# Building the filter's polynomials for two units in one block of matmuls

## The chip, the cores and the metric

The kernel runs on one core of a Trainium2 chip. Times are microseconds of device time from the start to the end of one execution; the median of three executions is given. The engines of the core are TensorE (PE, with its weight loads PEld), VectorE (DVE), ScalarE (ACT), GpSimd (POOL) and SyncE (SP), which issues most DMAs.

## What is computed

Two layers act on images of shape (4, 512, 512, 16), both on group-normalised input and with a residual. The first is a convolution through the frequency domain, the second a 3x3 cosine-similarity convolution. The change lies in how the filter of the first is made, for each of 16 x 16 pairs of input channel i and output channel j:

```python
a = jnp.pad(denumerator, ((0, 0), (0, 0), (1, 0), (1, 0)), constant_values=1.0)
b = jnp.pad(numerators, ((0, 0), (0, 0), (0, 0), (1, 0), (1, 0)), constant_values=0.0)
H_truncated = jnp.fft.rfft2(b, s=(l1, l2)) / jnp.fft.rfft2(a, s=(l1, l2))
h_truncated = jnp.fft.irfft2(H_truncated, s=(l1, l2))
H = jnp.fft.rfft2(h_truncated, s=(2 * l1, 2 * l2))
H_full = h0 + H[0]
```

Both a and b are polynomials of 9 x 9 coefficients in two variables, evaluated at 512 x 512 frequencies (256 of the second are kept). Their quotient is the filter, h0 is added by way of b + h0 a, and the result goes to the taps in space and on to 1024 x 1024 frequencies.

## The kernel before

The program has four stages in a row: the filter (`filter_phase`), the forward transform of the images, the product in the frequency domain, and the last stage with the inverse transform and the second layer. Beside the filter stage runs `image_stats`, statistics of the images on VectorE.

The filter stage works through a list `work` of 1024 units: output channel j, half h of the second frequency (128 of 256), input channel i, and kp, two of four blocks of 128 of the first frequency. The loop over v (L445) takes one unit a step and works on four units at once, each at a later point:

- `polynomials` (L321) makes a and b of unit v. First `quad` (L303) has multiplied the coefficients of four channels with the powers of the first frequency (L313) and copied the products to u (L315): a tile of 128 rows for a and one for b, in which each channel has a group of 32 rows (18 of them used: real and imaginary parts of nine coefficients). Channel i lies in group i % 4 of the tile for a, and in group (i % 4) ^ 1 of that for b. L329 multiplies those 18 rows by the powers of the second frequency, e2, for two blocks k: four matmuls a unit, each of 128 x 256 outputs, into two PSUM tiles pab0 (a) and pab1 (b). A float32 matmul is two instructions in the profile, so a unit has eight. ACT copies both tiles to SBUF (ab, L335) and squares a (sq, L337).
- `square` (L341, GpSimd) adds the squares to |a|^2 (dn). `product` multiplies b by a elementwise (m, L347, VectorE), takes the reciprocal of dn (L348, VectorE) and multiplies the crossed parts (x, L350 and L351, GpSimd).
- `terms` (L355, L356, GpSimd) puts real and imaginary part of the product together in m; `quotient` (L361, VectorE) multiplies them by 1/|a|^2 into sp and, for h = 0, puts in the special column z (L364).
- `taps` (L372) multiplies sp by dinv into PSUM (pg, four matmuls, eight instructions), and ACT copies the two parts into the stage tiles st (L377). After i = 15, kp = 1, SyncE stores the two stage tiles to memory (L383).

Each step also advances `odd` (L389) by one part: two matmuls (four instructions, L417) for the odd rows of a channel j that is already stored, whose copy is VectorE's (L423) and ACT's (L425) in turn, with loads ahead (L403) and stores (L426) by SyncE.

Buffers decide who may run ahead: PSUM has four banks for pab (L239), two a unit; two for pg, two for pt, pu and pz together; SBUF has two of each of ab, sq, dn, m and sp, one of x, and three stage tiles for the two of each j and h. The order of instructions on each engine is the framework's scheduler's, which starts from the written order and moves what is ready ahead: the statistics, written one of two bn_stats a step, stand at some eight a unit in places.

The step of the loop that calls these functions, and its functions, follow with line numbers.

Of the kernel before, what the change touches and what calls it, by code (L numbers as in the profile page):

```python
# [40 lines left out]
F32 = mybir.dt.float32  # L41
# [5 lines left out]
P = 128  # L47
N = 512
B = 4
C = 16  # L50
# [135 lines left out]
def load_const(nc, pool, cst, name, shape=None):  # L186
    src = cst[name]
    t = pool.tile(list(src.shape), F32, name=f"c_{name}")
    nc.sync.dma_start(out=t, in_=src)
    return t  # L190
# [38 lines left out]
def filter_phase(tc, cst, h0, num, den, g_d, beside):  # L229
    nc = tc.nc  # L230
    with ExitStack() as ctx:
# [7 lines left out]
        ps_ab = ctx.enter_context(tc.tile_pool(name="f_psab", bufs=4, space=PSUM))  # L239
# [4 lines left out]
        e2 = load_const(nc, cp, cst, "e2").rearrange("p (s h n) -> p s h n", s=2, h=2)  # L244
# [58 lines left out]
        def quad(sa, sb, iq):  # L303

            us = []
            for n, s in enumerate((sa, sb)):
                pu = ps_t.tile([P, N], F32, name=f"pu{n}", tag="t")  # L310
                for i in range(4):
                    at = 32 * (i ^ n)
                    nc.tensor.matmul(pu[at : at + 32], s[:, 4 * iq + i], e1, start=True, stop=True)  # L313
                u = wt.tile([P, N], F32, name=f"u{n}")
                nc.scalar.copy(u, pu)  # L315
                us.append(u)
            return us

        def polynomials(w):  # L321

            pp = [ps_ab.tile([P, 2, 2, P], F32, name=f"pab{n}", tag="ab") for n in range(2)]
            for k in range(2):
                k1 = (2 * w["kp"] + k) * P
                for n in range(2):
                    at = 32 * (w["i"] % 4 ^ n)
                    q = slice(at, at + 18)
                    nc.tensor.matmul(  # L329
                        pp[n][:, k].rearrange("p c n -> p (c n)"),  # L330
                        w["us"][n][q, k1 : k1 + P], e2[q, n, w["h"], :], start=True, stop=True,
                    )
            w["ab"] = [ew.tile([P, 2, 2, P], F32, name=f"ab{n}") for n in range(2)]
            for n in range(2):
                nc.scalar.copy(w["ab"][n], pp[n])  # L335
            w["sq"] = ew.tile([P, 2, 2, P], F32, name="sq")
            nc.scalar.activation(w["sq"], w["ab"][0], AF.Square)  # L337

        def square(w):
            w["dn"] = ew.tile([P, 2, P], F32, name="dn")  # L340
            nc.gpsimd.tensor_add(w["dn"], w["sq"][:, :, 0], w["sq"][:, :, 1])  # L341

        def product(w):

            a, b = w["ab"]
            w["m"] = ew.tile([P, 2, 2, P], F32, name="m")
            nc.vector.tensor_mul(w["m"], b, a)  # L347
            nc.vector.reciprocal(w["dn"], w["dn"])  # L348
            w["x"] = ew.tile([P, 2, 2, P], F32, name="x", bufs=1)
            nc.gpsimd.tensor_mul(w["x"][:, :, 0], b[:, :, 0], a[:, :, 1])  # L350
            nc.gpsimd.tensor_mul(w["x"][:, :, 1], b[:, :, 1], a[:, :, 0])  # L351

        def terms(w):
            m, x = w["m"], w["x"]
            nc.gpsimd.tensor_add(m[:, :, 0], m[:, :, 0], m[:, :, 1])  # L355
            nc.gpsimd.tensor_sub(m[:, :, 1], x[:, :, 1], x[:, :, 0])  # L356

        def quotient(w):
            sp = w["sp"] = ew.tile([P, 2, 2, P], F32, name="sp")
            for c in range(2):  # L360
                nc.vector.tensor_mul(sp[:, :, c], w["m"][:, :, c], w["dn"])  # L361
            if w["h"] == 0:
                kp = w["kp"]
                nc.vector.tensor_copy(sp[:, :, :, 0], w["z"][:, 2 * kp : 2 * kp + 2, :, w["i"]])  # L364

        def taps(w):

            kp, i, st = w["kp"], w["i"], w["st"]
            pg = ps_g.tile([P, 2, 2, 2 * 64], F32, name="pg")
            for k in range(2):  # L370
                for c in range(2):
                    nc.tensor.matmul(  # L372
                        pg[:, k].rearrange("p a x -> p (a x)"), w["sp"][:, k, c, :],
                        dinv[:, 2 * kp + k, c, :], start=(c == 0), stop=(c == 1),
                    )
            for a in range(2):
                nc.scalar.copy(  # L377
                    st[a][:, :, i].rearrange("p (q k x) -> p k q x", q=2, k=4)[:, 2 * kp : 2 * kp + 2],
                    pg[:, :, a].rearrange("p k (q x) -> p k q x", q=2),
                )  # L380
            if i == C - 1 and kp == 1:
                for a in range(2):
                    nc.sync.dma_start(  # L383
                        out=dram(g_d[w["h"]], None, a * G_ROW // 2 + w["j"] * 8 * C,
                                 [C * 8 * C, 64], [1, 8 * C]),
                        in_=st[a].rearrange("p (r e) i -> p r (e i)", e=8),
                    )
# [44 lines left out]
        def odds():  # L432

            for j in range(C):
# [2 lines left out]
                yield from odd(j)  # L437

        work = [dict(j=j, h=h, i=i, kp=kp)
                for j in range(C) for h in range(2) for i in range(C) for kp in range(2)]  # L440
        done = [0]
        rest = odds()
        polys = {0: weights(0)}
        us = quad(*polys[0][:2], 0)
        for v in range(len(work) + 3):  # L445
            next(rest)
            if v % 64 == 32 and v < len(work) - 64:
                polys[v // 64 + 1] = weights(v // 64 + 1)
            if v < len(work):
                w = work[v]  # L450
                if v % 8 == 0 and v:
                    us = ahead
                w["us"], w["z"] = us, polys[w["j"]][2]
                polynomials(w)
                if v % 8 == 4 and v + 4 < len(work):
                    g = (v + 4) // 8
                    ahead = quad(*polys[g // 8][:2], g % 4)
            first, second, third = (work[v - k] if 0 <= v - k < len(work) else None for k in (1, 2, 3))
            if first:
                square(first)  # L460
            if second:
                terms(second)
            if first:
                product(first)
            if second:
                quotient(second)
            if third:
                if third["i"] == 0 and third["kp"] == 0:
                    st = [stp.tile([P, N, C], F32, name=f"st{a}", tag="st") for a in range(2)]
                third["st"] = st  # L470
                taps(third)
                done[0] += 1
                third.clear()
            if v % 2:
                next(beside, None)
# [831 lines left out]
def body(tc, ins, cst, out):  # L1307
    g_d = [tc.dram_tile([P, G_ROW + PITCH], F32, name=f"g_d{r}") for r in range(4)]
    x_d = [tc.dram_tile([P, X_ROW + PITCH], F32, name=f"x_d{r}") for r in range(4)]
    y_d = [tc.dram_tile([P, Y_ROW + PITCH], F32, name=f"y_d{r}") for r in range(4)]  # L1310
    yw_d = [tc.dram_tile([C, N, N], F32, name=f"yw_d{b}") for b in range(B)]
    t_d = [[tc.dram_tile([N, P, C], F32, name=f"t_d{b}_{w}") for w in range(4)] for b in range(B)]
    with tc.tile_pool(name="s_mv", bufs=2 * B) as mp:
        mvs = []
        with tc.tile_pool(name="s_in", bufs=1) as xp:
            beside = image_stats(tc, xp, mp, ins["x"], mvs)
            filter_phase(tc, cst, ins["L0_conv_h0"], ins["L0_conv_numerators"][0],
                         ins["L0_conv_denumerator"], g_d, beside)
            for _ in beside:
                pass  # L1320
        forward_phase(tc, cst, ins["x"], mvs, x_d)
    conv_phase(tc, cst, g_d, x_d, y_d)
    last_phase(tc, cst, ins["x"], y_d, yw_d, t_d, ins["L1_conv_kernel"], ins["L1_conv_bias"],
               ins["L1_conv_radius"], out)
# [30 lines left out]
```

## Time and profile before

| | us |
|---|---|
| median of three runs | 19007.57 (19006.79 to 19023.34) |
| the profiled execution itself | 19054.31 |
| its span, first to last instruction | 19052.5 |
| last reciprocal of the filter stage (L348) starts at | 5669.8 |
| busy in the span: PE, DVE, ACT, POOL | 17293.1, 11398.8, 9747.4, 11564.3 |
| mean granted clock of TensorE in the span | 0.957 of full speed |

Busy times are sums over the whole span, in which four stages with different limits lie one behind the other. What an edit in the filter stage is worth has to be read from that stage alone: the same columns for a stretch of it, the order of time of each engine in it, and the waits. A timeline line has start, duration, engine, line of the program, operation, outputs and inputs by the program's names, shapes, and the number of instructions merged; in brackets the idle time of the engine before it, and what ended that. A busy TensorE is not a TensorE at its peak: matmuls are pipelined, so distances between starts are used here, not durations.

### The profile page before, as it was taken

How to read it: one execution, taken by the hardware profiler on the slowest of the kernel's cores; microseconds unless marked ns; L12 is line 12 of the kernel's file. 1: busy time of each engine (PE TensorE's matmuls, PEld its weight loads, DVE VectorE, ACT ScalarE, POOL GpSimd, SP SyncE). 2: the span in 40 equal slices, each digit the busy share in tenths (PEclk: the TensorE clock that was granted, in tenths of full speed). 3: DMA queues.
4: the chain of work that ended last, by engine and by line, in shares of the span. 5: the costliest groups of instructions: out<-in, count | busy, mean ns of one | idle time of the engine just before them, and what ended most of it. 6: DMA issues, size and time to landing. Idle time of an engine off the chain costs nothing. (4 is left out here: it accounts for less than half of the span.)

```text
span 19052.5 us, 536690 instructions
## 1 busy us (share of the span) xinstructions
PE 17293.1 (91%) x227020; PEld 12605.2 (66%) x227020; DVE 11398.8 (60%) x23961; ACT 9747.4 (51%) x17871; POOL 11564.3 (61%) x12445
## 2 busy tenths in 40 slices
PE   8899999999999988898888888888888888979999
PEld 5455555555554457777777777777777776868888
DVE  8877777777763335555555555555555554347656
ACT  4455555555552235555555555555555553107777
POOL 7577777777771126666666666666666664127655
PEclk7899999999999999999999999999999999999999
DMA  3755455555557668888888888888888887796321
GB/s 100 206 153 148 137 150 150 146 139 149 149 151 223 187 211 320 323 322 324 320 322 317 322 327 317 322 324 323 320 325 323 321 320 282 268 321 210 131 72 62
DMA packets 2918658, 4543.39 MB, mean 238 GB/s; under 512 B 117442, under 2 KB 2086300, under 8 KB 2809374
## 3 DMA queue, kind: packets, MB, share of 16 engines
q1 hardware_dynamic: 2686062, 3768.91, 58.5%
q0 software_dynamic: 174896, 605.89, 8.3%
q10 hardware_dynamic: 55296, 134.24, 2.1%
q8 instruction: 1789, 29.31, 0.6%
q14 instruction: 615, 5.04, 0.1%
HBM read 3031.23 MB, written 1477.31 MB: 237 GB/s over the span
## 5 line engine op out<-in xcount | busy, mean ns | idle before, releaser
L783 PE MATMUL pg<-c_dg,g 64*128 64x128 f32 x32832 | 2842.9, 291 | 320.9 <-ACT gh L683 159.5
L799 PE MATMUL pm<-xe,gh 128*32 128x64 f32 x131328 | 2403.4, 222 | 576.2 <-issue 353.1
L799 PEld LDWEIGHTS pm<-xe,gh 128*32 128x32 f32 x131328 | 2012.8, 110 | 1180.2 <-issue 996.4
L783 PEld LDWEIGHTS pg<-c_dg,g 64*128 64x128 f32 x32832 | 2283.2, 190 | 662.7 <-issue 262.5
L372 PE MATMUL pg<-c_dinv,sp 128*128 128x256 f32 x8192 | 2278.4, 426 | 294.3 <-ACT st L377 193.8
L828 DVE TENSOR_TENSOR z<-zq,pz 128x256 f32<-128x256 f32 x2052 | 862.0, 420 | 2617.2 <-ACT zq L827 2534.6
L348 DVE RECIPROCAL dn<-dn 128x256 f32<-128x256 f32 x1024 | 1790.8, 1749 | 778.3 <-POOL dn L341 778.0
L372 PEld LDWEIGHTS pg<-c_dinv,sp 128*128 128x128 f32 x8192 | 1609.9, 207 | 946.8 <-ACT st L377 215.3
L681 DVE COPY gh<-pg 128x512 f32<-128x512 f32 x2046 | 1410.5, 689 | 1294.1 <-PE pg L783 1289.6
L417 PE MATMUL pt<-ev_in,c_todd 128*128 128x512 f32 x4096 | 1970.1, 606 | 45.6 <-DMA ev_in<-g_d 27.0
L752 POOL TENSOR_TENSOR xu<-xe,c_late 128x256 f32<-128x256 f32 x2052 | 1393.4, 705 | 856.3 <-ACT xe L683 832.3
L335 ACT COPY ab<-pab 128x512 f32<-128x512 f32 x2048 | 1104.2, 592 | 1130.1 <-POOL m L355 333.3
L683 ACT COPY yf<-pm 128x512 f32<-128x512 f32 x2046 | 1210.5, 592 | 919.0 <-PE pm L799 904.3
L377 ACT COPY st<-pg 128x256 f32<-128x256 f32 x2048 | 1072.6, 623 | 1024.0 <-PE pg L372 619.3
L763 ACT COPY xe<-xl 64x1024 f32<-64x1024 f32 x513 | 538.8, 1050 | 1877.0 <-POOL xl L754 1877.0
L350 POOL TENSOR_TENSOR x<-ab,ab 128x256 f32<-128x256 f32 x1024 | 875.8, 855 | 933.6 <-ACT ab L335 907.0
L1208 PE MATMUL pc<-l_band,xn 128*128 128x160 f32 (+3 forms) x9024 | 1374.8, 309 | 65.0 <-DVE e_o L1255 64.0
L683 ACT COPY gh<-pg 128x512 f32<-128x512 f32 x2058 | 1201.2, 584 | 402.0 <-PE pg L783 393.6
L820 PE MATMUL pz<-c_ident,yf 128*128 128x128 f32 x8208 | 1378.2, 291 | 27.2 <-issue 25.4
L1208 PEld LDWEIGHTS pc<-l_band,xn 128*128 128x128 f32 x9024 | 1218.8, 197 | 224.7 <-issue 147.2
L329 PEld LDWEIGHTS pab<-c_e,u 18*128 18x128 f32 x8192 | 723.5, 188 | 809.5 <-ACT st L377 452.5
L417 PEld LDWEIGHTS pt<-ev_in,c_todd 128*128 128x128 f32 x4096 | 806.8, 198 | 669.9 <-issue 514.6
(195 smaller groups left out, 33846.4 us busy)
## 6 DMA issues: line engine op xcount, KB each, us to landing
xe<-xf_d SPq DMA_DIRECT2D x1026, 1536.0 KB, 10.3
g<-g_d SPq DMA_DIRECT2D x511, 1024.0 KB, 9.9
g_d<-st SPq DMA_DIRECT2D x64, 4096.0 KB, 34.3
ev_in<-g_d SPq DMA_DIRECT2D x1024, 256.0 KB, 4.8
g_d<-ot SPq DMA_DIRECT2D x1024, 256.0 KB, 2.9
xf_d<-xe POOLq DMA_DIRECT2D x513, 448.0 KB, 8.3
xf_d<-xl POOLq DMA_DIRECT2D x513, 448.0 KB, 5.3
x_d<-xo SPq DMA_DIRECT2D x128, 1024.0 KB, 5.1
```

The source lines that it names most:

```text
L335: nc.scalar.copy(w["ab"][n], pp[n])
L348: nc.vector.reciprocal(w["dn"], w["dn"])
L372: nc.tensor.matmul(pg[:, k].rearrange("p a x -> p (a x)"), w["sp"][:, k, c, :], dinv[:, 2 * kp + k, c, :], start=(c == 0), stop=(c == 1),)
L377: nc.scalar.copy(st[a][:, :, i].rearrange("p (q k x) -> p k q x", q=2, k=4)[:, 2 * kp : 2 * kp + 2], pg[:, :, a].rearrange("p k (q x) -> p ...
L417: nc.tensor.matmul(pt, todd[:, c, kc, hh * P : hh * P + P], ev[:, kc, c], start=(kc == 0), stop=(kc == 1),)
L681: nc.vector.tensor_copy(dst, src)
L683: nc.scalar.copy(dst, src)
L752: nc.gpsimd.tensor_mul(u[:, :, h, c], xe[:, :, h, 1 - c], bc(late[:, 1 + c], 2, [P, F, 2]))
L783: nc.tensor.matmul(pg[c][:, j % 4], g[half, j], dg[half], start=True, stop=True)
L799: nc.tensor.matmul(pm[32 * q : 32 * q + 32, g % 8], gh[:, f].rearrange("p c j -> p (c j)"), xe[:, :, f].rearrange("p t h c k -> p t (h c k ...
L820: nc.tensor.transpose(pz[:, t % 4].rearrange("p v q x -> p (v q x)"), y[:, at].rearrange("p g x -> p (g x)"), ident)
L1208: nc.tensor.matmul(pc[:, lo:hi, :].rearrange("p w j -> p (w j)"), xns[q][:, h * P + dh : h * P + dh + P], bands[dh][:, o : o + hi - lo, :] ...
```

## The change

The work list is put in another order: channels i and i ^ 2 stand side by side, and kp is outside of them. At every even step, `polynomials` now takes two units, allocates all four pab tiles, and issues their eight matmuls for k = 0 and then k = 1, in each k the two of the first unit and the two of the second. By the places of the rows, i, i ^ 1, i ^ 2 and i ^ 3, these four lie in the four groups of 32 rows. What came after the matmuls, the copies and the square on ACT, is a function `evict` of its own, called for one unit at every step, as before.

```diff
--- before.py
+++ after.py
@@ -318,19 +318,26 @@
-        def polynomials(w):
-            pp = [ps_ab.tile([P, 2, 2, P], F32, name=f"pab{n}", tag="ab") for n in range(2)]
+        def polynomials(pair):
+            for w in pair:
+                w["pp"] = [ps_ab.tile([P, 2, 2, P], F32, name=f"pab{n}", tag="ab") for n in range(2)]
             for k in range(2):
-                k1 = (2 * w["kp"] + k) * P
-                for n in range(2):
-                    at = 32 * (w["i"] % 4 ^ n)
-                    q = slice(at, at + 18)
-                    nc.tensor.matmul(
-                        pp[n][:, k].rearrange("p c n -> p (c n)"),
-                        w["us"][n][q, k1 : k1 + P], e2[q, n, w["h"], :], start=True, stop=True,
-                    )
+                for w in pair:
+                    k1 = (2 * w["kp"] + k) * P
+                    for n in range(2):
+                        at = 32 * (w["i"] % 4 ^ n)
+                        q = slice(at, at + 18)
+                        nc.tensor.matmul(
+                            w["pp"][n][:, k].rearrange("p c n -> p (c n)"),
+                            w["us"][n][q, k1 : k1 + P], e2[q, n, w["h"], :], start=True, stop=True,
+                        )
+        def evict(w):
             w["ab"] = [ew.tile([P, 2, 2, P], F32, name=f"ab{n}") for n in range(2)]
+            pp = w.pop("pp")
             for n in range(2):
                 nc.scalar.copy(w["ab"][n], pp[n])
             w["sq"] = ew.tile([P, 2, 2, P], F32, name="sq")
@@ -437,7 +444,8 @@
                 yield from odd(j)
         work = [dict(j=j, h=h, i=i, kp=kp)
-                for j in range(C) for h in range(2) for i in range(C) for kp in range(2)]
+                for j in range(C) for h in range(2) for i2 in range(0, C, 2) for kp in range(2)
+                for i in (i2 // 4 * 4 + i2 // 2 % 2, i2 // 4 * 4 + i2 // 2 % 2 + 2)]
         done = [0]
         rest = odds()
         polys = {0: weights(0)}
@@ -451,7 +459,11 @@
                 if v % 8 == 0 and v:
                     us = ahead
                 w["us"], w["z"] = us, polys[w["j"]][2]
-                polynomials(w)
+                if v % 2 == 0:
+                    pair = work[v : v + 2]
+                    pair[1]["us"] = us
+                    polynomials(pair)
+                evict(w)
                 if v % 8 == 4 and v + 4 < len(work):
                     g = (v + 4) // 8
                     ahead = quad(*polys[g // 8][:2], g % 4)
```

## The prediction

> **What bounds the kernel now.** The change lies in the filter stage alone, which the busy times in stretches place in the first 5700 us of the 19052.5 us span. I read its stretches first, then TensorE's timeline in one undisturbed stretch, then that of GpSimd, then the waits. The columns of the stretches are: stretch, length, busy us and instructions of PE, weight loads, DVE, ACT, POOL, granted clock, DMA share, GB/s.
> ```profile
> 110.00:400.00 290.00, 249.88 (x998) 160.64 (x996) 260.70 (x454) 142.83 (x284) 230.60 (x289) 0.72 0.32 87
> 1000.00:5600.00 4600.00, 4386.40 (x18754) 2602.75 (x18752) 3471.05 (x4454) 2601.71 (x4889) 3544.93 (x4412) 0.95 0.53 147
> 2104.71:2137.63 32.92, 32.92 (x141) 20.16 (x140) 25.18 (x32) 20.33 (x38) 27.52 (x34) 1.00 0.40 115
> 2137.63:2145.87 8.24, 8.24 (x37) 4.42 (x37) 6.34 (x7) 4.18 (x8) 7.83 (x12) 0.79 0.19 56
> ```
> From 1000 to 5600 us TensorE is busy 95%, no other engine over 77%. The trace has 849 reciprocals (one a unit) in it, so a unit takes 4600/849 = 5.42 us on average. The third line is seven units without a disturbance: 32.92/7 = 4.70 us each, TensorE busy throughout.
>
> TensorE's timeline (start, us, what) shows what fills 4.70 us, and, where the work list runs out, what a unit costs without its polynomials:
> ```profile
> 2109.41 1.13 PE L329 MATMUL pab<-c_e,u 18*128 18x256 f32 x8
> 2110.47 1.99 PE L372 MATMUL pg<-c_dinv,sp 128*128 128x256 f32 x8
> 2112.30 1.88 PE L417 MATMUL pt<-ev_in,c_todd 128*128 128x512 f32 x4
> 2114.11 1.13 PE L329 MATMUL pab<-c_e,u 18*128 18x256 f32 x8
> ...
> 5667.37 1.88 PE L417 MATMUL pt<-ev_in,c_todd 128*128 128x512 f32 x4
> 5669.09 1.89 PE L372 MATMUL pg<-c_dinv,sp 128*128 128x256 f32 x8
> 5670.81 1.88 PE L417 MATMUL pt<-ev_in,c_todd 128*128 128x512 f32 x4
> 5672.53 1.89 PE L372 MATMUL pg<-c_dinv,sp 128*128 128x256 f32 x8
> ```
> Start to start: polynomials 1.06, taps 1.83, odd rows 1.81, together 4.70. Without polynomials 1.72 + 1.72 = 3.44 us. So a block of polynomials costs TensorE 4.70 - 3.44 = 1.26 us, 0.20 of it in the neighbours' starts. Inside the block the trace has the eight instructions start at 2109.412, .418, .732, .738, .948, .954, 2110.163 and .170: four rounds of two that start 6 to 7 ns apart, the rounds 0.32, 0.216 and 0.216 us apart.
>
> The next limit is GpSimd:
> ```profile
> 2107.13 1.17 POOL L350 TENSOR_TENSOR x<-ab,ab 128x256 f32<-128x256 f32 x1 [1.93 <-ACT ab L335]
> 2108.26 0.74 POOL L351 TENSOR_TENSOR x<-ab,ab 128x256 f32<-128x256 f32 x1
> 2108.95 0.73 POOL L341 TENSOR_TENSOR dn<-sq 128x256 f32<-128x256 f32 x1
> 2109.63 0.74 POOL L355 TENSOR_TENSOR m<-m 128x256 f32<-128x256 f32 x1
> 2110.44 0.73 POOL L356 TENSOR_TENSOR m<-x 128x256 f32<-128x256 f32 x1
> 2111.83 0.82 POOL L350 TENSOR_TENSOR x<-ab,ab 128x256 f32<-128x256 f32 x1 [0.67 <-ACT ab L335]
> ```
> Its five operations go through without a pause and then wait for the copy of the next polynomials, which comes 0.07 us behind TensorE. From the start of x to the end of m it takes 4.04 us here and 4.14 and 4.29 in the next two units: 4.16, or 4.24 with the 0.08 us to the next start. GpSimd thus has only about 0.46 us of slack in a unit of 4.70.
>
> The waits from 1000 to 5600 us name what makes 4.70 into 5.42:
> ```profile
> POOL x L350 <- ACT ab L335: 753.3, 591, 11.3
> ACT st L377 <- DMA g_d<-st: 213.6, 27, 10.0
> PE pg L372 <- ACT st L377: 169.0, 27, 8.5
> ```
> Every 32 units the output stage waits about 8 us for a store, and all engines behind it (0.25 us a unit). Every eighth unit has the products of the next four channels (L313): 6.55 us at full clock, 8.24 in the fourth stretch above at a clock of 0.79.
>
> **What the Trainium skill says.** TensorE: Matmul & The Clock Gate, Part 3 (Packing small matmuls): matmuls on different groups of 32 rows run at once, start about 4 ns apart, and four such tiles of K=32, N=512 were measured 3.07 times as fast. The trace agrees for two row groups (6 to 7 ns). For four it shows only column groups: the L313 matmuls start at 2099.218, .225, .232, .238. Four row groups no line here shows. TensorEngine Tiling (Array Packing), Key Properties: a change of tiling mode drains the engine. The trace agrees: the last odd-row matmul to the first polynomial is 0.52 us where the next odd-row one would come at 0.43. GPSIMD Engine Reference, Key points: GpSimd shares its SBUF interfaces with VectorE, and contends with instructions of two SBUF inputs. The trace agrees: VectorE's quotient product (L361) has a minimum of 353 ns and a maximum of 991. The Clock Gate page, Part 1: the clock drops to half after windows of little activity and returns with it; here 0.72 from 110 to 400 us, where TensorE has no odd rows to do.
>
> **The change part by part.** *One block for two units.* 16 instructions in one block in place of two blocks of 8. If four row groups start together, it has four rounds as before and 2 x 6.5 ns more: a pair costs 4.703 + 3.44 + 0.013 = 8.16 us in place of 9.41. TensorE gains 1.25 us a pair, 0.62 a unit. The same 16 weight loads per pair lie within the block (eight take 0.73 of 1.13 us now, and loads in different row groups overlap). If only two start together, four more rounds of 0.216 come back, and 1.25 - 0.86 = 0.39 us a pair is left. That is the lower bound, for the drain is saved in any case; the upper is 1.25. I take 1.25.
>
> *Four banks at a time.* The pool has four banks and a pair takes all, so the block waits for the copies of both units of the pair before. Behind that wait on TensorE are the taps and odd rows; ACT's tap copies wait for them, and VectorE for its next free sp. With E the end of a block: ACT copies the first unit to E + 1.14, squares it to E + 1.8, copies taps to about E + 3.1, and copies the second unit to about E + 4.2, once GpSimd has released the older ab. TensorE wants the banks at E + 7.1 (8.16 - 1.06). Cover 2.9 us: cost nothing. If the scheduler puts the second copy behind the tap copy of the next unit, it ends about E + 7.6 and a pair loses 0.6 us, 0.3 a unit; that is the bound above. Below nothing it can also go: the second unit's polynomials wait in PSUM already, so GpSimd gets them without waiting for TensorE.
>
> *GpSimd becomes the limit.* TensorE's 4.08 us a unit is below GpSimd's 4.24. Its operations, VectorE's and ACT's are the same in number. I take 4.30: 4.24 and a little for more collisions with VectorE, whose quotient would fall beside the next x. Bounds: 4.08 (GpSimd's unhindered five times 0.73 would allow it) and 4.70 (nothing). The early stage, where TensorE is not the limit, went at some 4.8 us a unit, but with half clocks and statistics on VectorE; this speaks for the upper side.
>
> *Eighth units and stores.* The eighth unit's extra 1.85 us stays on TensorE: 0.23 a unit, 4.31 in all, so it remains on the path partly; I put 0.06 a unit as hidden. The 8 us for a store stay. The order of channels (i and i ^ 2 side by side) changes no instruction count: the quads still change every eighth unit, i = 15, kp = 1 is still last and issues the two stores, and no DMA is moved past another on SP, ACT or POOL. Cost nothing: only the order inside the quad differs.
>
> *The sum.* In units 160 to 1023 (from 1000 us on): 864 x (4.70 - 4.30) = 346, and 864 x 0.06 = 52. In the first 160, where VectorE does the statistics (609 of 700 us busy from 300 to 1000), about 0.03 us each, 5. Together 403, say 400 us. The later stages only start sooner. The profiled execution took 19054.31 us (span 19052.5 and 1.8 around it), 47 us or 0.25% over the median 19007.57; the difference is taken from both: 18654 for such an execution, 18610 for the median.
>
> **The rivals.**
> *VectorE and GpSimd bind earlier*, at 4.50 us a unit: 864 x 0.20 = 173, with some 15 more: 18820. For: the early stage's 4.8, VectorE's 991 ns when contended. Against: three GpSimd cycles of 4.04 to 4.29 in this very stage.
> *The whole saving arrives*: GpSimd goes at 4.08, and 864 x 0.62 = 536 and 15 more: 18460. For: an unhindered cycle is 5 x 0.73 = 3.65 with small gaps. Against: collisions are there already.
> *Four groups don't start together*: 0.39 us a pair, 0.19 a unit, 864 x 0.19 = 164: 18840. For: only two were seen. Against: four column groups do.
> *Slower by the clock*: TensorE has gaps at the pair's block, waiting for the fourth bank, and the clock halves. One such stretch costs 8.24 - 6.55 = 1.69 us now (the taps take 3.50 us in place of 1.99). Once in each pair: 8.16 + 1.69 = 9.85 against 9.41, 0.22 a unit, 864 x 0.22 = 190 slower: 19200. It decides from 1.25/1.69 = 0.74 halvings a pair. For: 0.72 in the early stage. Against: at 4.30 TensorE still works 95% of a unit, and today's halvings follow gaps near 1 us.
>
> **How the numbers follow.** Forecast 0.52 (18610, with its own range 18500 to 18740), earlier bound 0.18, whole saving 0.12, two at a time 0.06, clock 0.12. The range 18430 to 18880 takes in the first four; left out are the clock and some 0.06 of tails. A measurement of this kernel tells about 0.2% (38 us) from no change. Within it I put 0.02 of the earlier bound and 0.03 of the clock: same 0.05. Slower is 0.09, faster 0.86.
>
> **What would show it.** Right: 16 L329 instructions a block, in four rounds of four about 7 ns apart, a block of about 1.15 us every two units; GpSimd's wait for ab near nothing; units of about 4.3 us between disturbances; store waits as before. Wrong: eight rounds; blocks that wait for ab copies; clock below 0.9 from 1000 to 5600 us; GpSimd cycles of 4.5 us or more.

## The result and the profile after

The changed kernel takes 19053.78 us (median of 20 executions, 19011.07 to 19099.3) beside 19009.13 us of the kernel before (20 executions, 18967.88 to 19045.35): a ratio of 1.002 with a 95% interval of 1.0013 to 1.0027, so slower by 0.2%. The forecast was 18610, and its range ended at 18880.

The profiled execution of the changed kernel took 19023.83 us (span 19022.1), 30 us under its median; that of the kernel before was 45 us over its own. Spans are therefore compared here for the filter stage alone. The busy times in stretches, with the columns used before (stretch, length, PE, weight loads, DVE, ACT, POOL, clock, DMA share, GB/s):
```profile
110.00:400.00 290.00, 213.00 (x1004) 134.02 (x1003) 259.75 (x465) 148.41 (x290) 227.01 (x288) 0.77 0.35 94
1000.00:5600.00 4600.00, 4094.07 (x18733) 2409.82 (x18732) 3716.36 (x4545) 2522.52 (x4887) 3635.89 (x4413) 0.92 0.53 148
```
From 1000 to 5600 us TensorE is busy 292 us less than before (89% of the stretch, not 95%), with the same number of instructions to within 0.2%. VectorE is busy 245 us more. Of these, 22 us are 80 instructions of the statistics, which in the kernel before had ended by 1000 us; the rest is that operations changed in length: one instruction of sp takes 821 ns in the mean (574 before), while m takes 699 (868 before) and the copy of z 190 (370 before). GpSimd is busy 91 us more for the same number of operations. The stretch holds 847 reciprocals where it held 849, so nothing of TensorE's gain has come out.

TensorE's timeline shows the new block:
```profile
2505.31 1.15 PE L333 MATMUL pab<-c_e,u 18*128 18x256 f32 x16
...
2513.67 1.15 PE L333 MATMUL pab<-c_e,u 18*128 18x256 f32 x16
...
2516.69 1.98 PE L424 MATMUL pt<-ev_in,c_todd 128*128 128x512 f32 x4
2519.34 2.34 PE L379 MATMUL pg<-c_dinv,sp 128*128 128x256 f32 x8 [0.68 <-DVE sp L368]
```
Sixteen instructions take 1.15 us where eight took 1.13, and they start in four rounds of four (the first at 2505.307, .314, .321 and .327, 6 to 7 ns apart as two groups were before): the four groups of rows do start together. But in the last line TensorE stands still 0.68 us, and what it waits for is VectorE's sp. GpSimd's and VectorE's timelines of the same time tell why:
```profile
2513.36 0.73 POOL L357 TENSOR_TENSOR x<-ab,ab 128x256 f32<-128x256 f32 x1
2514.05 0.91 POOL L358 TENSOR_TENSOR x<-ab,ab 128x256 f32<-128x256 f32 x1
2515.38 1.24 POOL L348 TENSOR_TENSOR dn<-sq 128x256 f32<-128x256 f32 x1 [0.42 <-DVE sp L368]
2516.58 0.72 POOL L362 TENSOR_TENSOR m<-m 128x256 f32<-128x256 f32 x1
2517.38 0.73 POOL L363 TENSOR_TENSOR m<-x 128x256 f32<-128x256 f32 x1
...
2520.21 1.24 POOL L348 TENSOR_TENSOR dn<-sq 128x256 f32<-128x256 f32 x1 [0.43 <-DVE sp L368]
```
```profile
2513.49 1.74 DVE L368 TENSOR_TENSOR sp<-m,dn 128x256 f32<-128x256 f32 x2
2515.34 0.69 DVE L354 TENSOR_TENSOR m<-ab,ab 128x512 f32<-128x512 f32 x1
2515.95 0.69 DVE L430 COPY ot<-pt 128x512 f32<-128x512 f32 x1
2516.65 1.75 DVE L355 RECIPROCAL dn<-dn 128x256 f32<-128x256 f32 x1
2518.32 1.74 DVE L368 TENSOR_TENSOR sp<-m,dn 128x256 f32<-128x256 f32 x2
...
2521.48 1.75 DVE L355 RECIPROCAL dn<-dn 128x256 f32<-128x256 f32 x1 [0.62 <-POOL dn L348]
```
GpSimd no longer waits for ab in such units. It waits 0.42 us before dn, for sp (L368): dn has two buffers, and the one that is due is still read by the quotient of the unit two before. VectorE does a reciprocal, then the quotient of the unit before it. So there is a ring: dn starts at 2515.38, its reciprocal at 2516.65 (1.27 later), the quotient of the unit before at 2518.32 (1.67 later), and the next dn when that is over, at 2520.21 (1.89 later). Together 4.83 us, more than TensorE's 4.70 of before. VectorE's own work is not what sets this pace: in the unit shown it has no pause, but in the next one, whose odd-row copy is ACT's, it stands still 0.62 us for dn (the last line), and from reciprocal to reciprocal that unit takes 4.83 us too. Two of the three terms are stretched: the two instructions of sp, which run beside the two x, take 1.74 us (one of them by itself took at least 353 ns), and dn, which runs beside VectorE's m, takes 1.24 (0.73 by itself). Over the stretch from 1000 to 5600 us the median of one sp instruction went from 411 to 881 ns, and that of dn from 727 to 1237 ns (shortest, median and longest in ns; the kernel before first):
```profile
L361 DVE TENSOR_TENSOR sp<-m,dn x1698: 353/411/991, 1001.0 to 5597.5; 128x256 f32<-128x256 f32 x189
L341 POOL TENSOR_TENSOR dn<-sq x849: 714/727/1321, 1002.3 to 5599.1; 128x256 f32<-128x256 f32 x170
L368 DVE TENSOR_TENSOR sp<-m,dn x1695: 348/881/2356, 999.7 to 5598.2; 128x256 f32<-128x256 f32 x189
L348 POOL TENSOR_TENSOR dn<-sq x848: 716/1237/1249, 1005.3 to 5599.2; 128x256 f32<-128x256 f32 x170
```

The waits from 1000 to 5600 us confirm it for the whole stage:
```profile
POOL x L357 <- ACT ab L342: 477.4, 123, 11.7
...
POOL dn L348 <- DVE sp L368: 263.3, 593, 4.5
...
ACT st L384 <- DMA g_d<-st: 206.4, 27, 9.7
```
```profile
POOL dn L341 <- DVE sp L361: 54.3, 127, 0.7
```
The last line is that of the kernel before. There GpSimd waited 591 times for ab, with 753.3 us in all, and 127 times for sp; now it is 123 times and 593 times. The stalls by stores are what they were (206.4 us now and 213.6 before).

**The sums by time.** Undisturbed units take 4.83 us instead of 4.70. The stretches around quads and stores, in which TensorE catches up at 8.2 to 8.4 us a pair (8.36 above, from 2505.31 to 2513.67), became shorter by as much: from unit 160 to the last reciprocal it is 4667.7 us now and 4670.5 before. What the trace shows as lost lies earlier: unit 160 starts at 1022.1 us instead of 999.3, and the last reciprocal at 5689.8 instead of 5669.8. That is 20 us of the 45 between the medians. I haven't located the other 25: after the last reciprocal the profiled executions of all kernels here differ by up to 77 us (13305 to 13383), and the changed kernel's was 50 us shorter than that of the kernel before. From 400 to 1000 us the waits of after, and below them those of before, show where the early part goes:
```profile
ACT ab L342 <- DVE stats L556: 160.7, 25, 9.8
...
DVE stats L556 <- DMA xs<-in_x: 93.6, 28, 8.0
...
ACT st L384 <- DVE stats L556: 27.9, 8, 6.1
```
```profile
ACT st L377 <- DVE stats L544: 96.7, 34, 7.8
ACT ab L335 <- DVE stats L544: 80.0, 16, 7.3
...
DVE stats L544 <- DMA xs<-in_x: 38.5, 21, 7.2
```
VectorE stands at the statistics, which wait for their loads. These are issued by ACT, where they queue behind copies that themselves wait for VectorE. ACT's waits for the statistics alone would not tell the two kernels apart: with its tap copies st (27.9 us now, 96.7 before) they come to 188.6 and 176.7 us. What has grown is the wait of the statistics for their loads.

### The profile page after: what moved, and what is told of

Same layout as the page of the kernel before. It is cut to its first block, busy times and chain, and to the rows that moved or that the text cites. A ratio compares the mean times of both kernels' runs of the same rounds, so it can differ in the third digit from the quotient of the medians.

```text
span 19022.1 us, 536659 instructions
## 1 busy us (share of the span) xinstructions
PE 16896.8 (89%) x227020; PEld 12348.7 (65%) x227020; DVE 11628.5 (61%) x23961; ACT 9657.3 (51%) x17871; POOL 11658.3 (61%) x12445
## 5 line engine op out<-in xcount | busy, mean ns | idle before, releaser
L379 PE MATMUL pg<-c_dinv,sp 128*128 128x256 f32 x8192 | 2348.5, 434 | 456.5 <-DVE sp L371 188.2
L379 PEld LDWEIGHTS pg<-c_dinv,sp 128*128 128x128 f32 x8192 | 1677.9, 214 | 1329.5 <-issue 496.6
L368 DVE TENSOR_TENSOR sp<-m,dn 128x256 f32<-128x256 f32 x2048 | 1542.1, 791 | 183.1 <-PE pg L379 181.6
L348 POOL TENSOR_TENSOR dn<-sq 128x256 f32<-128x256 f32 x1024 | 1124.2, 1098 | 381.2 <-DVE sp L368 340.7
```

The costliest lines, as they stand in the source:

```text
L379: nc.tensor.matmul(pg[:, k].rearrange("p a x -> p (a x)"), w["sp"][:, k, c, :], dinv[:, 2 * kp + k, c, :], start=(c == 0), stop=(c == 1),)
```

## The experiments

A ratio is to the kernel before, timed on the same chip, with its 95% interval in brackets.

**Is it the four groups?** The pair is i and i + 1, which lie in the same two groups of rows:
```diff
-                for i in (i2 // 4 * 4 + i2 // 2 % 2, i2 // 4 * 4 + i2 // 2 % 2 + 2)]
+                for i in (i2, i2 + 1)]
```


> The changed kernel with the pair i, i + 1 in place of i, i ^ 2: both units lie in the same two groups of rows, so that only two matmuls run at once and a pair's block has eight rounds, 0.86 us more (9.02 a pair on TensorE, 4.51 a unit). Theory (TensorE is not the limit after the change): units stay at 4.83, time within 0.3% of the changed kernel. Rival (TensorE is still the limit through its block): 0.43 us a unit more, 864 x 0.43 = 370 us slower than the changed kernel.

Measured: 19068.43 us, 1.003 (1.0018 to 1.0041). The block takes 2.00 us and TensorE in its catch-up 9.01 us a pair (2503.93, 2512.94, 2521.95), as the prediction's bound of 0.39 us a pair gives (9.41 - 0.39 = 9.02). Yet undisturbed units take 4.82 to 4.83 us, the same as with four groups. So 0.85 us of TensorE a pair more or less hardly reaches the time: it is not TensorE that limits the undisturbed units of the changed kernel.

**Is it the order of the channels?** The polynomials of before, one unit a time, with the work list of the change:
```diff
         work = [dict(j=j, h=h, i=i, kp=kp)
-                for j in range(C) for h in range(2) for i in range(C) for kp in range(2)]
+                for j in range(C) for h in range(2) for i2 in range(0, C, 2) for kp in range(2)
+                for i in (i2 // 4 * 4 + i2 // 2 % 2, i2 // 4 * 4 + i2 // 2 % 2 + 2)]
```


> The kernel before with the work list of the change, but a block of its own for each unit, as before. Theory (the order of the channels is free): units at 4.70, time within 0.2% of before. Rival (the order costs something by itself, in the quads or in the stage tiles): slower by what the changed kernel is, 0.2% or more.

Measured: 19000.12 us, 0.9997 (0.9989 to 1.0005). The order costs nothing, as predicted.

**Is it the ring through dn?** A third buffer, in the changed kernel and in that of before:
```diff
-            w["dn"] = ew.tile([P, 2, P], F32, name="dn")
+            w["dn"] = ew.tile([P, 2, P], F32, name="dn", bufs=3)
```


> The changed kernel with a third buffer for dn. Theory (a ring through dn: with two buffers the sum of squares of a unit waits for the quotient of the unit two before, and the ring dn, reciprocal, quotient takes 1.24 + 1.67 + 1.75 + 0.17 = 4.83 us while its members collide with x and m): the ring opens, undisturbed units fall from 4.83 us to between 4.1 and 4.4, and the kernel is 250 to 450 us faster than before. Rival (VectorE and GpSimd share one road and are full at 4.83, whatever the buffers): units stay at 4.8, time within 0.3% of the changed kernel. Rival (TensorE still bounds, by the four banks or the clock): the same.

> The kernel before with a third buffer for dn and nothing else. Theory: TensorE holds it at 4.70 us a unit and GpSimd waits for it, so the ring is not the limit here: units stay at 4.70, time within 0.3% of before. Rival (the dn buffer is a gain by itself and has nothing to do with the change): over 0.5% faster.

Measured: 19621.91 us, 1.0319 (1.0305 to 1.0333), in the changed kernel; 18988.63 us, 0.9984 (0.9977 to 0.999), in that of before. In the kernel before, the buffer brings next to nothing, as expected. The large loss in the changed one answers no question about the ring, for the edit did a second thing: with a free buffer the framework's scheduler put reciprocals of later units ahead of m (L354) in VectorE's order, and GpSimd then waits for m. Three lines of VectorE's timeline, and the first of the waits from 1000 to 5600 us:
```profile
2499.82 1.75 DVE L355 RECIPROCAL dn<-dn 128x256 f32<-128x256 f32 x1 [1.98 <-POOL dn L348]
2503.47 1.75 DVE L355 RECIPROCAL dn<-dn 128x256 f32<-128x256 f32 x1 [1.90 <-POOL dn L348]
...
2505.94 0.68 DVE L354 TENSOR_TENSOR m<-ab,ab 128x512 f32<-128x512 f32 x1
```
```profile
POOL m L362 <- DVE m L354: 1134.7, 384, 5.8
```
In the changed kernel with two buffers that wait was 35.8 us in all. The units go at 4.02 and 7.36 us in turn, 6.02 in the mean. To test the ring, VectorE's order has to be held. An edge that only orders (it makes no instruction wait for another engine) keeps m, then the reciprocal of the same unit, then the quotient of the unit before; once with three buffers, once with two:
```diff
+        chain = []
+        def in_turn(ins):
+            if chain:
+                tc.add_manual_dep(ins.ins, chain[-1].ins.name,
+                                  mybir.DependencyInfo(mybir.DependencyClass.NoSync, mybir.DependencyReason.DATA),
+                                  reason="in turn")
+            chain.append(ins)
...
-            w["dn"] = ew.tile([P, 2, P], F32, name="dn")
+            w["dn"] = ew.tile([P, 2, P], F32, name="dn", bufs=3)
...
-            nc.vector.tensor_mul(w["m"], b, a)
-            nc.vector.reciprocal(w["dn"], w["dn"])
+            in_turn(nc.vector.tensor_mul(w["m"], b, a))
+            in_turn(nc.vector.reciprocal(w["dn"], w["dn"]))
...
-                nc.vector.tensor_mul(sp[:, :, c], w["m"][:, :, c], w["dn"])
+                in_turn(nc.vector.tensor_mul(sp[:, :, c], w["m"][:, :, c], w["dn"]))
```


> The changed kernel with a third buffer for dn, and VectorE's issue order held as the changed kernel has it (product m, reciprocal, quotient of the unit before), since the third buffer alone let the scheduler put reciprocals of later units ahead of m, for which GpSimd then waited. The only thing that differs from the changed kernel is that GpSimd's sum of squares no longer waits for the quotient of two units before. Theory (the ring dn, reciprocal, quotient is what holds 4.83): units at 4.1 to 4.4, 250 us or more faster than before. Rival (VectorE and GpSimd are full at 4.83 through their shared road): units stay above 4.7.

> The changed kernel with VectorE's issue order held as in the run beside it, but two buffers for dn. Theory: the order is the one that the changed kernel already has, so units stay at 4.83 and the time within 0.3% of the changed kernel. Rival (holding the order is itself what gains or loses): as the run beside it.

Measured: 18879.63 us, 0.994 (0.9927 to 0.9953), with three buffers; 19047.19 us, 1.002 (1.0013 to 1.0028), with two. Holding the order alone does nothing; the buffer takes off 0.9%, so the ring is a cause. Undisturbed units fall from 4.83 to 4.62 in the mean for h = 0 (4.70 and 4.54 in turn) and to 4.55 for h = 1 (4.63 and 4.47), the mean from unit 160 on from 5.41 to 5.26. They stop short of TensorE's 4.08 and of my expectation of 4.1 to 4.4, so a second limit lies behind the first. VectorE's timeline in that kernel:
```profile
2504.31 1.74 DVE L364 RECIPROCAL dn<-dn 128x256 f32<-128x256 f32 x1
2505.97 1.22 DVE L377 TENSOR_TENSOR sp<-m,dn 128x256 f32<-128x256 f32 x2
2507.29 1.03 DVE L363 TENSOR_TENSOR m<-ab,ab 128x512 f32<-128x512 f32 x1
2508.24 0.68 DVE L439 COPY ot<-pt 128x512 f32<-128x512 f32 x1
2508.94 1.75 DVE L364 RECIPROCAL dn<-dn 128x256 f32<-128x256 f32 x1
...
2517.83 0.69 DVE L363 TENSOR_TENSOR m<-ab,ab 128x512 f32<-128x512 f32 x1
...
2520.65 0.74 DVE L377 TENSOR_TENSOR sp<-m,dn 128x256 f32<-128x256 f32 x2
```
From one reciprocal to the next (4.63 us) VectorE has no pause. The last two lines, taken beside a disturbance, are m and the two sp when they meet nothing: 0.69 and 0.74 us; above they take 1.03 and 1.22, in other units up to 1.75. VectorE's own work, stretched, fills the unit.

**Where the early loss comes from.** The loads of the statistics are issued by SyncE in place of ACT, in the changed kernel and in that of before:
```diff
-        nc.scalar.dma_start(out=t, in_=x[b, h * P : (h + 1) * P, w * P // 2 : (w + 1) * P // 2, :])
+        nc.sync.dma_start(out=t, in_=x[b, h * P : (h + 1) * P, w * P // 2 : (w + 1) * P // 2, :])
```


> The changed kernel with the loads of the image statistics issued by SyncE in place of ACT. In units 64 to 160 the changed kernel is some 20 us later than before, and VectorE's statistics wait longer for these loads (93.6 against 38.5 us from 400 to 1000 us). Theory: the loads stand behind copies on ACT that wait for VectorE, which stands behind the statistics; without this, units 64 to 160 take 20 to 60 us less than in the changed kernel and the rest is as it was. Rival (the 20 us are the ring's, too): nothing changes before 1000 us.

> The kernel before with the statistics' loads issued by SyncE. Theory (the loads behind ACT's copies cost more where the copies wait longer, so in the changed kernel more than in the one before): it gains less than the changed kernel did by the same edit (70 us), some 30 us. Rival (the loads' place costs both the same): 60 to 80 us.

Measured: 18976.18 us, 0.9987 (0.998 to 0.9995), in the changed kernel; 18974.21 us, 0.9975 (0.9967 to 0.9983), in that of before. Unit 160 starts at 952.4 us (1022.1 with the loads on ACT), and at 959.2 (999.3). VectorE's wait for these loads is 9.4 us in both. By that start the edit is worth 70 us in the changed kernel and 40 in that of before: the queue of ACT was a wait in both, and a longer one after the change. With it gone, the changed kernel is 6.8 us ahead at that start. In the whole the medians then differ by 2 us; the two ratios, taken on different chips, differ by 0.0012, and their intervals just overlap.

**Is TensorE's gain real?** The second crossed product is left out, after and before:
```diff
-            nc.gpsimd.tensor_mul(w["x"][:, :, 1], b[:, :, 1], a[:, :, 0])
...
-            nc.gpsimd.tensor_sub(m[:, :, 1], x[:, :, 1], x[:, :, 0])
+            nc.gpsimd.tensor_sub(m[:, :, 1], m[:, :, 1], x[:, :, 0])
```


> The changed kernel without the second crossed product on GpSimd (L358); the difference takes the imaginary part of m in its place, so the filter's imaginary parts are not computed as the reference has them. GpSimd has four operations a unit in place of five. Theory (TensorE's saving is there, and the elementwise work of GpSimd and VectorE hides it): undisturbed units fall from 4.83 to 4.1 to 4.3, near TensorE's 4.08, and the kernel is 300 to 600 us faster than before. Rival (something else of the change, the four banks or the clock, holds it): units stay above 4.6.

> The kernel before with the same operation left out (L351). Theory (TensorE holds it at 4.70): undisturbed units stay at 4.70, time at most 0.5% below before. Rival (GpSimd already is part of the limit in the kernel before): units fall as in the run beside it, and the two differ by less than 0.5%.

Measured: 18568.07 us, 0.9775 (0.976 to 0.979), for the changed kernel; 18916.65 us, 0.9945 (0.9933 to 0.9958), for that of before. Once elementwise work is taken away, the change is worth 349 us, 1.8%. Before, undisturbed units stay at 4.70 to 4.74, as a kernel does that waits for TensorE; after, they fall to 4.30, with 4.95 in the mean instead of 5.35. TensorE's timeline in a catch-up of the changed one:
```profile
2510.31 1.15 PE L333 MATMUL pab<-c_e,u 18*128 18x256 f32 x16
...
2518.47 1.15 PE L333 MATMUL pab<-c_e,u 18*128 18x256 f32 x16
```
8.16 us a pair, to the hundredth what the prediction had worked out.

**What is the second limit?** The edits of the run with the third buffer and the held order, and on top of them that of the runs without a crossed product:
```diff
-            nc.gpsimd.tensor_mul(w["x"][:, :, 1], b[:, :, 1], a[:, :, 0])
...
-            nc.gpsimd.tensor_sub(m[:, :, 1], x[:, :, 1], x[:, :, 0])
+            nc.gpsimd.tensor_sub(m[:, :, 1], m[:, :, 1], x[:, :, 0])
```


> The changed kernel with the third dn buffer and the held order of VectorE (as in the run at 18880), and without the second crossed product (x has one half only, and m- takes the imaginary part of m in its place, so the numbers computed are not the reference's). With the second product in, undisturbed units stood at 4.54 to 4.70 us; without it and with two dn buffers (18568) at 4.30. Theory: the 4.6 was the sum of what VectorE's two-input operations and GpSimd need of one shared way (three GpSimd operations under sp, sp and m in 1.75 + 1.24 us, the other two alone 1.46, together 4.45), and the 4.30 was the ring through two dn buffers. One operation less and a ring opened leave 3.7 of shared way, and TensorE's 8.16 a pair is the limit: units of 4.08 to 4.15, some 100 to 170 us under 18568, 18400 to 18470. Rival: VectorE's own order (stretched m, reciprocal, stretched sp, its part of the odd-row copies) is what held 4.6 and 4.30: it is no shorter here, units stay at 4.30 or above, 18540 to 18600. Second rival: what is left above 4.08 are the disturbances by stores and quads, not the undisturbed unit: units of 4.08, but the mean hardly below that of 18568 (4.95), 18520 or more.

Measured: 18600.72 us, 0.9794 (0.9779 to 0.9808), not under 18568 but at the upper end of the first rival's band and inside the second's. The theory's time was not reached. Undisturbed units take 3.76 and 4.62 us in turn, 4.19 in the mean, so the ring gave 0.11 us a unit; but the mean from unit 160 on is 5.00, so the disturbed units give it back. GpSimd now waits for VectorE's m more than for anything else (684.5 us in 712 waits from 1000 to 5400 us), and VectorE again runs without a pause between disturbances. This speaks for VectorE's own order as the second limit, and against the sum of the two engines' operations as I had taken it (3.7 us), but it doesn't show the one: VectorE's order is as long as it is because most sp still take 1.2 to 1.4 us the pair, beside GpSimd's operations, where a pair that meets none takes 0.73. Nor does it part the two rivals: how much of the 5.00 is VectorE, and how much TensorE at quads and stores, stays open.

**A version that beats both.** The third dn buffer, the held order and the statistics' loads on SyncE together, with the edits shown above:

> The changed kernel with three things together: a third dn buffer, VectorE's issue order held, and the statistics' loads issued by SyncE. Theory: the gains add, 165 us from the first two and 70 us from the third against the changed kernel, so about 18815 us, 1.0% faster than before. Rival (the loads only move the statistics, and the ring's room is the same slack): no faster than the first two alone, 18880.

Measured: 18832.08 us, 0.9906 (0.9893 to 0.992). Against the changed kernel's 19053.78 the parts gave 174 and 78 us alone, and 222 together, so they nearly add (the runs are from chips on which the kernel before differs by up to 6 us). Beside the kernel before with the same loads on SyncE, timed on the same chip, it is 142 us faster; the kernel before with the loads and a third buffer together wasn't run. A fourth stage tile, which would bear on the stalls by stores, wasn't tried.

## Why the prediction was wrong

- *The block for two units: right.* Four groups start together, 1.15 us a block, 8.16 us a pair where TensorE limits (the runs without a crossed product); with two groups 9.01.
- *Four banks at a time: right.* TensorE's stops in undisturbed units are not for the copies of ab but for sp; from 1000 to 5600 us no matmul of pab waits for a copy of ab.
- *The order of channels and the stores at nothing: right* (19000 us; store waits of 206 and 214 us).
- *"GpSimd becomes the limit ... I take 4.30": this step failed.* The 4.24 us were GpSimd's time for a unit's work, and they were nearly right: after the change its five operations take 4.33 us (0.73 + 0.91 + 1.24 + 0.72 + 0.73). But I costed each engine by itself and took the longest. Between GpSimd and VectorE runs a ring through the two buffers of dn, and its length, 1.27 + 1.67 + 1.89 = 4.83 us, I didn't add up. Before, it was hidden: TensorE's wait came last, so x and with it all that follows started late, and dn's buffer was free by then (54.3 us of waits). The rows were in the profile: dn, the reciprocal, the quotient's 991 ns, and two dn buffers. Added up with the stretched rows they would have given 1.2 + 1.7 + 2 x 0.9, some 4.7 us, and so no gain. The choice of the stretched rows is hindsight.
- *Eighth units: partly right.* The disturbed stretches do become shorter: the mean less the undisturbed unit was 5.41 - 4.70 = 0.71 and is 5.41 - 4.83 = 0.58. That is 0.13 a unit rather than 0.06, and it pays back just what the undisturbed units lose.
- *The first 160 units: wrong in sign.* I put 5 us of gain; the trace shows 22.8 of loss, by the queue of the statistics' loads on ACT. With the loads on SyncE it is gone: the changed kernel is then 6.8 us ahead.
- *The rivals.* The mechanism of the first, VectorE and GpSimd bind earlier, is what happened, at 4.83 us rather than 4.50. My argument against it, three GpSimd cycles of 4.04 to 4.29, had been measured while TensorE held GpSimd back, so it couldn't tell what GpSimd does when it isn't held back. The clock's rival is not needed for the undisturbed units: the granted clock fell from 0.95 to 0.92 from 1000 to 5600 us, but the run with three buffers and the held order has 0.92 as well and is faster than before (0.994), with the same blocks of polynomials. The clock records have 133 spells of half speed in that stretch, 751 us in all, where before there were 94, 451 us in all. That is 0.31 a pair in place of 0.22; the prediction's sum would have turned at 0.74. What they cost in the stretches around quads and stores stays open. That today's spells "follow gaps near 1 us" was misread: 50 of the 94 come with no gap of TensorE in the 7 us ahead of them, each 1.5 to 2.9 us after the start of a quad's products (L313).

The ring was there to be seen. It stands in the profile of the kernel before, in the early stage, where TensorE has no odd rows to do:
```profile
211.54 1.74 DVE L361 TENSOR_TENSOR sp<-m,dn 128x256 f32<-128x256 f32 x2
...
213.42 1.24 POOL L341 TENSOR_TENSOR dn<-sq 128x256 f32<-128x256 f32 x1 [0.43 <-DVE sp L361]
...
214.70 1.75 DVE L348 RECIPROCAL dn<-dn 128x256 f32<-128x256 f32 x1 [0.62 <-POOL dn L341]
...
216.37 1.76 DVE L361 TENSOR_TENSOR sp<-m,dn 128x256 f32<-128x256 f32 x2
```
From sp to dn it takes 1.88 us, to the reciprocal 1.28, to the next sp 1.67: 4.83 us, with dn waiting for sp. From 110 to 400 us dn waits for sp 21 times. Not every unit there is such a lap; in others VectorE is filled up by the statistics. But the prediction had these units as "some 4.8 us", and put them down to half clocks and to the statistics alone.

## What to carry to other kernels

When an edit frees the engine that bounds a stage, the next limit need not be the next busiest engine: follow each buffer from its writer through its readers back to its next writer, add up the durations with the stretched ones that the trace shows, and divide by the units that one lap advances. Durations and cycles read while another engine sets the pace are those of operations kept apart by that pace; take the upper end of what the trace shows. And an added buffer can change the order that a scheduler chooses, so hold the order when only the buffer is to be tested.

## What the hardware showed that I had not expected

- In the kernel before, from 2000 to 3000 us, VectorE's product of 128 x 256 elements (one instruction of sp) took 0.36 to 0.41 us where no GpSimd operation ran at the same time, and 0.83 us in the mean, up to 0.98, where one of GpSimd's x ran beside it throughout. GpSimd's dn took 0.71 to 0.74 us with VectorE idle, and up to 1.32 us beside VectorE's m. Even VectorE's copy of 4 columns went from 0.17 us to 0.58 (the median beside x). The reciprocal (1.74 to 1.76 us) and VectorE's copies from PSUM (0.63 to 0.69) didn't get longer, and neither did GpSimd's two sums of m, which ran beside the reciprocal (0.71 to 0.74).
- So two engines that are each busy under 81% of a stage can bound it: from 1000 to 5600 us of the changed kernel VectorE is busy 81%, GpSimd 79% and TensorE 89%, and none of the three is full.
